# A two-layer network on one core: the order of the second layer's end is rewritten (rows, convolution, pairs, scatters, sums)

## The chip, the core and the metric

The kernel runs on one core of a Trainium2 chip. The metric is the device time of one execution in microseconds (us), shown as the median of several executions. Five engines work in parallel, each through its own queue in order: TensorE (PE; its weight loads are listed as PEld), VectorE (DVE), ScalarE (ACT), GpSimd (POOL) and SyncE (SP), which here only starts transfers. POOL starts the transfers that follow a list of indices. All times inside an execution are counted from the start of the span of the profiled execution.

## What is computed

Four sequences of 1024 tokens with 256 channels in float32 pass through two layers. Layer 0 is causal latent attention with 16 heads and a mixture of 16 experts, two for each token. The change does not touch it. Layer 1, cut to what matters:

```python
# attention: relu, cubed and normalised q and k, kv product, 3-tap convolution over tokens
q = _norm_last(_norm_last(relu(q) + EPS) ** 3)          # the same for k
kv = einsum('bhnd,bhne->bhde', k, v)
z = 1.0 / (einsum('bhnd,bhd->bhn', q, k.sum(axis=2)) + EPS)
out = einsum('bhnd,bhde,bhn->bhne', q, kv, z)
xp = pad(out, ((0, 0), (1, 1), (0, 0)))
out = out + xp[:, 0:N] * w[:, 0] + xp[:, 1:N+1] * w[:, 1] + xp[:, 2:N+2] * w[:, 2] + b_dwc
x = x + ga * (einsum('bnc,oc->bno', out, w_proj) + b_proj)
# experts: one of eight for each token
h = layernorm(x) * (1 + cb) + sb
probs = softmax(h @ router_w + router_b)
x = x + gb * max(probs) * (h @ expert_w[argmax] + expert_b[argmax])
```

## The kernel before

`attention1` goes through five rounds, b = 0 to 4. In a round `front(b)` (layer norm, k and v, the kv products, q) and `back(b - 1)` (the products `ps_o` L1574, their normalisation `on` L1580, transposes `ps_oT` L1589 into `o`, the convolution `y` L1601, the projections `ps_pr` L1609, the sum into x L1614) are advanced in turn. After each turn `k.around.step(pieces, rides)` advances work of the experts that lies beside: *tasks* such as `rows(b)` (statistics of the layer norm, normalised rows `h`, router logits) and `sort(p)`, and *riders* such as `send(p)`. A round's pace says how many sixths of a piece one turn carries: `(6, 8, 6, 6, 12)[b]`, and one ride goes with each step unless another number is given.

The tokens are sorted by expert in three parts: part 0 is the sequences 0 and 1, part 1 is sequence 2 and part 2 sequence 3. `sort(p)` (L882 on) finds each row's place (`index`, L933) and the experts' offsets (`ps_expert` L949). `send(p)` loads rows back from memory (`hs`, L1870) and scatters them 128 at a time into `sorted` (L964), 16 scatters for part 0, 8 for each of the others. The sorted rows are then worked on in 25 pairs of tiles, 11 + 7 + 7. A pair loads `xs` (256 KB, L1008, SP's queue), transposes it (`ps_xT` L1923), copies it out (`xT`, ACT, L1927 for part 0, L1930 with a scale and a shift for the others), multiplies it with its expert's weights (`ps_y` L1938), adds the bias (L1944), for parts 1 and 2 the gate (L1946), and stores `results` (L1947, SP). `combine(p)` gathers the rows back in the order of the tokens (`ys`, L974, POOL, six buffers), scales them (part 0 on ACT, L2002, then gate and sum on DVE, L2007 and L2008; the others in one DVE operation, L1996) and stores `out_dram` (L2010).

The order on each engine comes from the order in which the program gives out instructions and from priorities; `k.pin` fixes an instruction's place among the pinned ones. `k.anchor` names a matmul behind which scatters and gathers are paced. Riders and tasks of parts 0 and 1 run between later pairs, with `k.around.step(2, 2)` after each pair. `count_sums` (L499) checks softmax sums in three passes through `good` tiles, which take buffers with the tag "xs" (six of them, the same as the loads of the pairs); it is given out when part 1's pairs end. `out_of_bounds` (L512) reduces that check with a matmul (`ps_good` L521) when part 2's pairs end.

Of the kernel before, what the change touches and what calls it, by code (L numbers as in the profile page):

```python
# [8 lines left out]
F32 = mybir.dt.float32  # L9
I32 = mybir.dt.int32  # L10
AF = mybir.ActivationFunctionType
ALU = mybir.AluOpType
# [488 lines left out]
def count_sums(k, pool):  # L501

    recs = [k.recs.rearrange("p n i j -> p (n i j)")]
    recs += [k.recs1[:, i].rearrange("p b t h -> p (b t h)") for i in range(2)]
    inverse = 1.0 / SUM_HI, 1.0 / SUM_LO
    for i, (rec, (low, high)) in enumerate(zip(recs, (inverse, (SUM_LO, SUM_HI), inverse))):
        good = pool.tile([P, 8 * B * H], F32, tag="xs", name="good", bufs=6)
        count_within(k, good, rec, low, high, k.good[:, i : i + 1])

# [333 lines left out]
class Sorting:  # L843
# [38 lines left out]
    def sort(self, sel, pool, index, offset):  # L882
# [50 lines left out]
        nc.vector.tensor_scalar(index, rows, 0.0, float(self.most * P - 1), ALU.max, ALU.min)  # L933
        yield 1
# [26 lines left out]
    def scatter(self, rows, buffer, index):  # L961

        tc = self.k.tc
        i = self.k.nc.gpsimd.indirect_dma_start(  # L964
            out=buffer.ap, out_offset=bass.IndirectOffsetOnAxis(ap=index, axis=0),
            in_=rows, in_offset=None, bounds_check=self.most * P - 1, oob_is_err=False,
        ).ins
        for other in buffer.writers:
            tc.declare_no_dep(i, other, reason="their rows are others")
        buffer.writers.append(i)  # L970
        self.paced(i)
# [473 lines left out]
def attention1(ctx, k, a, after_batch=lambda b: None):  # L1445
# [22 lines left out]

    nc.vector.tensor_scalar(dw[:, :, 1], dw[:, :, 1], 1.0, None, ALU.add)
# [86 lines left out]

    def back(b):
        kv, qT = kvs.pop(b), qTs.pop(b)
# [9 lines left out]
        for q in range(2):  # L1568
# [25 lines left out]
            nc.vector.tensor_tensor(xs, xs, bcast(bg, 1, 4), ALU.add)  # L1594
            yield
        for cc in range(CC):
            nc.scalar.activation(
                y[:, cc], o[:, cc, 1 : N + 1], AF.Identity, bias=db[:, cc, :], scale=dw[:, cc, 1:2]
            )
            for j in (0, 2):  # L1600
                nc.vector.scalar_tensor_tensor(  # L1601
                    y[:, cc], o[:, cc, j : N + j], dw[:, cc, j : j + 1], y[:, cc], ALU.mult, ALU.add
                )
            yield
# [12 lines left out]
    k.misc = ps_m  # L1617
    for b in range(B + 1):
        while b == HB and k.awaited in k.around.tasks:
            k.around.step()  # L1620
        todo = ([front(b)] if b < B else []) + ([back(b - 1)] if b else [])
        pace = (6, 8, 6, 6, 12)[b]
        n = 0
        while todo:
            todo = [g for g in todo if next(g, k) is not k]
            n += pace
            k.around.step(n // 6)
            n %= 6
        if b:
            after_batch(b - 1)  # L1630
# [153 lines left out]
class Experts1:  # L1784


    def __init__(self, k, a, out):
# [19 lines left out]
        self.sent = set()  # L1807
# [38 lines left out]
    def sort(self, p):  # L1846
# [12 lines left out]
        yield from sorting.sort(sel, rt, index, offset)  # L1859
        k.around.riders.append(self.send(p, index))  # L1860
        self.state[p] = index, offset, part

    def send(self, p, index):
# [10 lines left out]
        for i in range(len(pairs)):  # L1874
            hs = coming.pop(0)
            if i + 2 < len(pairs):
                coming.append(fetch(*pairs[i + 2]))
            for n in (2 * i, 2 * i + 1):
                self.sortings[p].scatter(hs[:, n % 2], k.sorted1[p], index[:, 0, n : n + 1])
                yield  # L1880
        self.sent.add(p)

    def run(self, early):

        k = self.k
        nc = k.nc
        work = self.back = self.stack.enter_context(
            k.tc.tile_pool(name="f1_work", bufs=2, reuse_waits="tile")
        )
        ps_x = self.stack.enter_context(  # L1890
            k.tc.tile_pool(name="f1_ps_x", bufs=4, space=PSUM, reuse_waits="tile")
        )
        ps_o = self.stack.enter_context(
            k.tc.tile_pool(name="f1_ps_o", bufs=4, space=PSUM, reuse_waits="tile")
        )
        k.misc = ps_x

        pairs = [
            (p, list(range(g, min(g + 2, s.tiles))))
            for p, s in enumerate(self.sortings)  # L1900
            for g in range(0, s.tiles, 2)
        ]
        coming = []

        def fetch(n):

            for p, tiles in pairs[n + len(coming) : n + 5]:
                if p not in self.sent:
                    break
                xs = work.tile([P, 2, C], F32, tag="xs", name="xs", bufs=6)  # L1910
                k.sorted1[p].load(xs[:, : len(tiles)], tiles)
                coming.append(xs)

        def tiles_of(p, tiles, xs):

            n = len(tiles)
            at = self.sortings[p].offsets(
                self.state[p][1], tiles, [mybir.EngineType.PE, mybir.EngineType.DVE]
            )
            ps = ps_x.tile([P, 2, CC, P], F32, tag="m", name="ps_xT")  # L1920
            for j in range(n):
                for cc in range(CC):
                    nc.tensor.transpose(ps[:, j, cc], xs[:, j, cc * P : (cc + 1) * P], k.ident)  # L1923
            xT = work.tile([P, 2, CC, P], F32, tag="xT", name="xT", bufs=3)
            b = PARTS[p][0] if len(PARTS[p]) == 1 else None
            if b is None:
                nc.scalar.copy(xT[:, :n], ps[:, :n])  # L1927
            else:
                for cc in range(CC):
                    nc.scalar.activation(  # L1930
                        xT[:, :n, cc], ps[:, :n, cc], AF.Identity,
                        bias=k.modF[:, cc, b : b + 1], scale=k.modF[:, 2 + cc, b : b + 1],
                    )
            yield
            po = ps_o.tile([P, 2, C], F32, tag="o", name="ps_y")
            for j in range(n):
                for cc in range(CC):
                    k.anchor = nc.tensor.matmul(  # L1938
                        po[:, j], lhsT=xT[:, j, cc], rhs=self.we[:, cc, bass.ds(at[j], C)],
                        start=cc == 0, stop=cc == CC - 1,  # L1940
                    ).ins
            y = work.tile([P, 2, C], F32, tag="y", name="y", bufs=3)
            for j in range(n):
                nc.vector.tensor_tensor(y[:, j], po[:, j], self.be[:, bass.ds(at[j], C)], ALU.add)  # L1944
            if b is not None:
                nc.vector.tensor_tensor(y[:, :n], y[:, :n], bcast(self.gate[:, b], 1, n), ALU.mult)  # L1946
            nc.sync.dma_start(k.results1[p].part(tiles), y[:, :n])  # L1947

        again, before = None, None
        for n, (p, tiles) in enumerate(pairs):  # L1950
            if p not in self.sent and before is not None:
                next(before, None)
                before = None
            while p not in self.sent:
                k.around.step(1, 2)
            fetch(n)
            now = tiles_of(p, tiles, coming.pop(0))
            next(now)
            if before is not None:
                next(before, None)  # L1960
            before = now
            if n + 1 == len(pairs) or pairs[n + 1][0] != p:
                next(before, None)
                before = None
                if early and p + 2 == len(PARTS):
                    count_sums(k, work)
                if early and p + 1 == len(PARTS):
                    again = out_of_bounds(k, work, ps_x)
                k.around.tasks.append(self.combine(p))
            k.around.step(2, 2)  # L1970
        k.around.drain()
        self.stack.close()
        return again

    def combine(self, p):
        k, work = self.k, self.back
        nc = k.nc
        index, _, part = self.state[p]
        most = self.sortings[p].nt

        def fetch(n):
            ys = work.tile([P, C], F32, tag="ys", name="ys", bufs=6)
            self.sortings[p].gather(ys, k.results1[p], index[:, 0, n : n + 1])
            return ys

        coming = []
        for n in range(4):
            coming.append(fetch(n))
            yield 0.5
        for n in range(most):  # L1990
            j = n % 2
            b, t = PARTS[p][n // NT], n % NT
            ys = coming.pop(0)
# [9 lines left out]
            if n + 4 < most:  # L2003
                coming.append(fetch(n + 4))
            if j == 1 and len(PARTS[p]) > 1:
                xs = k.x[b][:, t - 1 : t + 1]
                nc.vector.tensor_tensor(y, y, bcast(self.gate[:, b], 1, 2), ALU.mult)  # L2007
# [10 lines left out]
def two_layers(ctx: ExitStack, tc: tile.TileContext, a: dict, out: bass.AP):  # L2018
# [56 lines left out]
    def stages(first, second, early):  # L2075
# [22 lines left out]
        with ExitStack() as s, tc.using_default_side("right"):  # L2098
# [3 lines left out]
            second(s, k, a, *([after_attention1] if early else []))  # L2102
# [84 lines left out]
```

## Time and profile before

| what | us |
|---|---|
| median of 3 executions | 1086.05 |
| lowest and highest | 1083.16, 1089.41 |
| the profiled execution | 1087.63 |
| its span | 1085.8 |

| moments of the second layer in the profiled execution | us |
|---|---|
| kv products of rounds 1, 2, 3 on DVE (L1548) start | 826.4, 881.6, 934.2 |
| `y` of the convolution of batches 1, 2, 3 ends | 856.4, 906.1, 959.3 |
| `index` of the first sort | 926.2 |
| the 16 scatters of part 0 on POOL | 927.2 to 957.5 |
| first `xs` load issued | 959.1 |
| the last projections | 960.5 to 969.5 |
| scatters of part 2 | 996.4 to 1006.5 |
| gathers of part 0 / part 1 / part 2 | 1010.8 to 1033.0 / 1039.2 to 1050.3 / 1065.1 to 1075.3 |
| last `ps_y` ends | 1059.7 |

The profiled execution lies 1.58 us above the median; 1.83 us of its time lie outside its span. One reads the two tables together: the first says what is to be explained, the second where in the span each step of the end stands. Medians from issue to landing are 4.0 us for `xs`, 3.7 for `ys` and 3.4 for a store to `out_dram`.

### The profile page before, as it was taken

Reading aid. Unit: us, or ns where it says so; the run is one execution under the profiler, and the core shown is the slowest. Engines: PE = TensorE matmul, PEld = TensorE weight load, DVE = VectorE, ACT = ScalarE, POOL = GpSimd, SP = SyncE. Lnnn points to the kernel's source line nnn. Section 1 sums busy time; section 2 is a strip of 40 time slices with the busy share of each in tenths; the row PEclk is TensorE's granted clock in tenths of the full one; section 3 lists DMA queues with packets and bytes.
Section 4 is the critical chain, followed back from the end, with each engine's and each line's share of the span. In section 5 each row is a group of like instructions: output and inputs, shape, how many; then the busy total and the mean of one; then the engine's idle time right before and its main releaser. Section 6 shows DMA issues by size and latency. Waiting matters only on the chain.

```text
span 1085.8 us, 18090 instructions
## 1 busy us (share of the span) xinstructions
PE 945.7 (87%) x6072; PEld 559.8 (52%) x6072; DVE 620.4 (57%) x1987; ACT 602.5 (55%) x959; POOL 336.0 (31%) x528
## 2 busy tenths in 40 slices
PE   4899999999999999889679989986997989858760
PEld 2434434443443434335568878874464656547550
DVE  5822235422465155413676767993899968564572
ACT  0368655765477555775555657766654745523430
POOL 2013211311232234663004615612550100553632
PEclk9999999999999999999899999998999899989875
DMA  6995000100010001552825556624223201458764
GB/s 206 358 346 179 1 1 6 40 1 1 1 64 1 1 30 54 201 215 78 317 88 170 197 177 189 196 75 144 67 65 148 88 2 39 141 170 264 240 205 130
DMA packets 97142, 132.89 MB, mean 122 GB/s; under 512 B 8536, under 2 KB 84216, under 8 KB 96528
## 3 DMA queue, kind: packets, MB, share of 16 engines
q1 hardware_dynamic: 84656, 97.27, 26.9%
q0 software_dynamic: 11776, 33.57, 9.9%
q8 instruction: 52, 0.85, 0.3%
q10 hardware_dynamic: 608, 0.79, 0.3%
q14 instruction: 50, 0.41, 0.1%
HBM read 67.85 MB, written 63.75 MB: 121 GB/s over the span
## 4 chain that ended last, share of the span: by engine, by line
PE 63%; DVE 19%; issue 5%; DMA 5%; ACT 4%; POOL 1%; SPq 1%; DVEq 0%; ACTq 0%; POOLq 0%
PE ps_s L388 13%; PE ps_av L453 12%; PE ps_qk L364 6%; PE ps_y L1312 5%; PE ps_h L1247 4%; PE ps_v L349 3%; PE ps_out L427 3%; PE ps_pr L1609 3%; PE ps_y L1938 3%; PE ps_q L1537 2%; PE ps_k L1511 2%; DVE y L1601 2%; DMA ys<-results,index 2%; PE ps_lnT L1057 1%; DVE st L1258 1%
## 5 line engine op out<-in xcount | busy, mean ns | idle before, releaser
L396 ACT ACTIVATE pT<-ps_s 128x1024 f32<-128x1024 f32 x288 | 279.3, 1022 | 169.7 <-PE ps_s L388 167.2
L399 POOL TENSOR_SCALAR_AFFINE_SELECT pT<-pT 128x256 f32<-128x256 f32 x256 | 104.2, 431 | 328.4 <-ACT pT L396 323.7
L388 PE MATMUL ps_s<-qT,kT 32*128 32x512 f32 (+3 forms) x1536 | 178.8, 523 | 0.1
L453 PE MATMUL ps_av<-pT,v 128*32 128x512 f32 (+3 forms) x1536 | 165.2, 497 | 9.4 <-DVE turned L411 5.6
L964 POOL DMA_INDIRECT sorted<-hs,index x96 | 96.2, 1002 | 144.9 <-PE ps_y L1312 73.0
L974 POOL DMA_INDIRECT ys<-results,index x96 | 102.7, 1070 | 119.0 <-DMA results<-y 43.6
L388 PEld LDWEIGHTS ps_s<-qT,kT 32*128 32x128 f32 x1536 | 74.5, 185 | 95.5 <-issue 72.8
L453 PEld LDWEIGHTS ps_av<-pT,v 128*32 128x32 f32 x1536 | 40.6, 108 | 104.0 <-issue 58.7
L1247 PE MATMUL ps_h<-w,xT 128*128 x352 | 82.1, 386 | 6.5 <-DVE mv L1259 3.8
L1312 PE MATMUL ps_y<-w,act 128*128 x352 | 83.7, 392 | 4.2 <-DVE rs_seed L84 2.8
L411 DVE STREAM_TRANSPOSE turned<-ps_av 128x512 f32<-128x512 f32 x32 | 22.8, 712 | 98.9 <-PE ps_av L453 98.6
L1312 PEld LDWEIGHTS ps_y<-w,act 128*128 128x128 f32 x352 | 67.7, 197 | 14.0 <-ACT act L1295 4.8
L1247 PEld LDWEIGHTS ps_h<-w,xT 128*128 128x128 f32 x352 | 66.2, 193 | 15.9 <-issue 4.2
L1295 ACT ACTIVATE act<-ps_hT,gain 128x128 f32<-128x128 f32 x176 | 63.6, 463 | 16.9 <-PE ps_hT L1286 16.8
L1270 ACT ACTIVATE hid<-hid,nmr,rstd 128x256 f32<-128x256 f32 x88 | 47.5, 603 | 39.4 <-DVE nmr L1263 39.2
L1511 PE MATMUL ps_k<-wqkv,hT 128*128 128x512 f32 x128 | 61.9, 603 | 3.6 <-DMA wqkv<-in_wqkv_dram 2.8
L1938 PE MATMUL ps_y<-we,xT 128*128 x200 | 53.0, 412 | 10.6 <-ACT xT L1930 8.4
L371 DVE COPY qT<-ps_qk 128x512 f32<-128x512 f32 x16 | 11.0, 688 | 81.8 <-PE ps_qk L364 81.8
L103 DVE BATCH_NORM_STATS2 ln_st<-x 128x6 f32<-128x256 f32 x128 | 49.2, 407 | 0.5
L1255 DVE TENSOR_TENSOR hid<-ps_h,b 128x256 f32<-128x256 f32 x88 | 33.9, 415 | 26.6 <-PE ps_h L1247 21.5
L1938 PEld LDWEIGHTS ps_y<-we,xT 128*128 128x128 f32 x200 | 38.2, 204 | 20.1 <-ACT xT L1930 11.6
L374 DVE TENSOR_SCALAR kT<-ps_qk,par 128x512 f32<-128x512 f32 x32 | 22.5, 745 | 37.0 <-PE ps_qk L364 37.0
(223 smaller groups left out, 1499.4 us busy)
## 6 DMA issues: line engine op xcount, KB each, us to landing
xs<-sorted SPq DMA_DIRECT2D x69, 256.0 KB, 3.8
results<-y SPq DMA_DIRECT2D x69, 256.0 KB, 3.0
sorted<-zero SPq DMA_DIRECT2D x2, 6016.0 KB, 20.1
rows_in<-h SPq DMA_DIRECT2D x16, 512.0 KB, 2.9
hs<-rows_in POOLq DMA_DIRECT2D x32, 256.0 KB, 3.5
w<-in_w_dram SPq DMA_DIRECT2D x8, 1024.0 KB, 11.3
x<-in_x_dram SPq DMA_DIRECT2D x4, 1024.0 KB, 6.5
b<-in_b_dram SPq DMA_DIRECT2D x2, 2048.0 KB
```

The costliest lines, as they stand in the source:

```text
L364: nc.tensor.matmul(ps, lhsT=w[:, cc, g * P : (g + 1) * P], rhs=hT[:, cc, hf * 512 : (hf + 1) * 512], start=cc == 0, stop=cc == CC - 1,)
L388: k.anchor = nc.tensor.matmul(pair[hh // 2][:, hh % 2, c0 : c0 + w], lhsT=kTs[o][rows, kb * P : (kb + 1) * P], rhs=qT[rows, q1 - w : q1], ...
L396: nc.scalar.activation(pT, ps, AF.Exp, scale=1.0 / L**0.5)
L399: nc.gpsimd.affine_select(out=pT[:, :, c0 : c0 + P], in_=pT[:, :, c0 : c0 + P], compare_op=ALU.is_ge, fill=0.0, base=0, pattern=[[0, 2], [ ...
L453: nc.tensor.matmul(po[32 * hh : 32 * hh + 32, 512 - w :], lhsT=vs[b % 2][:, kb, 8 * g + 2 * hh + o, :], rhs=exps[b, g, o, u][hh // 2][:, h ...
L964: i = self.k.nc.gpsimd.indirect_dma_start(out=buffer.ap, out_offset=bass.IndirectOffsetOnAxis(ap=index, axis=0), in_=rows, in_offset=None, ...
L974: self.paced(self.k.nc.gpsimd.indirect_dma_start(out=rows, out_offset=None, in_=buffer.ap, in_offset=bass.IndirectOffsetOnAxis(ap=index, a ...
L1247: mm = nc.tensor.matmul(ph[:, j], lhsT=xTs[i // 2][:, j, cc], rhs=w1[:, cc, bass.ds(at[i + j], C)], start=cc == 0, stop=cc == CC - 1,)
L1295: o = nc.scalar.activation(act[:, j, cc], pt[:, j, cc], AF.Gelu, bias=gain[:, 1, cc, t : t + 1], scale=gain[:, 0, cc, t : t + 1],)
L1312: mm = nc.tensor.matmul(po[:, j], lhsT=acts[i // 2][:, j, cc], rhs=w2[:, cc, bass.ds(at[i + j], C)], start=cc == 0, stop=cc == CC - 1,)
L1511: k.anchor = nc.tensor.matmul(ps, lhsT=hT[:, cc, t * P : (t + 1) * P], rhs=wqkv[:, cc, C:], start=cc == 0, stop=cc == CC - 1,).ins
L1938: k.anchor = nc.tensor.matmul(po[:, j], lhsT=xT[:, j, cc], rhs=self.we[:, cc, bass.ds(at[j], C)], start=cc == 0, stop=cc == CC - 1,).ins
```

## The change

1. The addition of one to the middle tap, `dw`, is given out in `back(0)` instead of ahead of the rounds.
2. In the round b = 2 nothing is advanced beside before turn 8, and then at pace 8. In b = 3 the pace is 9. From b = 3 on two riders go with each step.
3. The last batch's convolution is done in halves of 511 and 513 tokens, each inside the loop over halves of the queries, ahead of the next half's products.
4. `beside` is called after each turn of the last round (b = 4). Once part 0 is sent, it loads rows and works on three pairs in turns 8, 9 and 10, in two buffers of the tag "hT" and in the PSUM banks with the tag "p".
5. `sort` calls `ready()` when `index` is written, ahead of the experts' offsets, and this starts `send(p)`. The last part's sender goes ahead of all other riders and isn't paced. `around.step(3.5, 0)` ahead of the pairs and the list `pieces` set how many pieces follow the first pairs.
6. `count_sums` gives out one pass after each of part 0's pairs from the seventh on, and its tiles have the tag "out".
7. The gathers are riders of their own (24 `ys` buffers, three rides after each pair). All combines, all stores to `out_dram` and `out_of_bounds` are given out behind the last pair.

```diff
@@ count_sums
-        good = pool.tile([P, 8 * B * H], F32, tag="xs", name="good", bufs=6)
+        good = pool.tile([P, 8 * B * H], F32, tag="out", name="good")
         count_within(k, good, rec, low, high, k.good[:, i : i + 1])
+        yield
@@ Sorting.sort
         nc.vector.tensor_scalar(index, rows, 0.0, float(self.most * P - 1), ALU.max, ALU.min)
+        ready()
         yield 1
@@ Sorting.scatter
-        self.paced(i)
+        if not at_once:
+            self.paced(i)
@@ attention1
-    nc.vector.tensor_scalar(dw[:, :, 1], dw[:, :, 1], 1.0, None, ALU.add)
...
+    def convolve(o, y, lo, hi):
+        for cc in range(CC):
+            nc.scalar.activation(
+                y[:, cc, lo:hi], o[:, cc, 1 + lo : 1 + hi], AF.Identity,
+                bias=db[:, cc, :], scale=dw[:, cc, 1:2],
+            )
+            for j in (0, 2):
+                nc.vector.scalar_tensor_tensor(
+                    y[:, cc, lo:hi], o[:, cc, j + lo : j + hi], dw[:, cc, j : j + 1], y[:, cc, lo:hi],
+                    ALU.mult, ALU.add,
+                )
+            yield
...
+            if b == B - 1:
+                for _ in convolve(o, y, *((0, N // 2 - 1), (N // 2 - 1, N))[q]):
+                    pass
             yield
...
+        if b < B - 1:
+            yield from convolve(o, y, 0, N)
...
+    k.bank = lambda name: ps_p.tile([P, 2, C], F32, tag="p", name=name)
+    k.spare = lambda: work.tile([P, CC, N], F32, tag="hT", name="spare")
...
-        pace = (6, 8, 6, 6, 12)[b]
+        pace, first = ((6, 0), (8, 0), (8, 7), (9, 0), (12, 0))[b]
         n = 0
+        turn = 0
         while todo:
             todo = [g for g in todo if next(g, k) is not k]
-            n += pace
-            k.around.step(n // 6)
+            turn += 1
+            if turn > first:
+                n += pace
+            k.around.step(n // 6, 1 + b // (B - 1))
             n %= 6
+            if b == B:
+                fill(turn)
@@ the experts of layer 1
-        yield from sorting.sort(sel, rt, index, offset)
-        k.around.riders.append(self.send(p, index))
+        riders = k.around.riders
+        yield from sorting.sort(
+            sel, rt, index, offset,
+            lambda: riders.insert(0 if p + 1 == len(PARTS) else len(riders), self.send(p, index)),
+        )
...
+    def beside(self, turn):
+        if 0 not in self.sent or turn > 10:
+            return
+        if self.space is None:
+            xs, other = (self.k.spare().rearrange("p c (n d) -> p (c n) d", d=2 * C) for _ in range(2))
...
+            self.space, self.most = space, 3
+        self.fetch()
+        if 8 <= turn <= 10:
+            self.pair()
+        if turn == 10:
+            self.products()
...
+        counts = count_sums(k, work) if early else iter(())
+        pieces = [0, 1.5, 3.5, 2.5, 2, 0, 1] if early else []
+        if early:
+            around.step(3.5, 0)
+        while self.done < len(self.pairs):
+            p = self.pairs[self.done][0]
+            if p not in self.sent:
+                self.products()
+            while p not in self.sent:
+                around.step(1, 2)
+            self.pair()
+            if p == 0 and self.done > 6:
+                next(counts, None)
+            if self.done == len(self.pairs) or self.pairs[self.done][0] != p:
+                around.riders.append(self.gathers(p))
+            around.step(pieces.pop(0) if pieces else 2, 3)
+        for _ in counts:
+            pass
+        again = out_of_bounds(k, work, ps_x) if early else None
+        while around.riders:
+            around.step(0)
+        around.tasks += [self.combine(p) for p in range(last + 1)]
+        around.drain()
...
+    def gathers(self, p):
+        index = self.state[p][0]
+        for n in range(self.sortings[p].nt):
+            ys = self.back.tile([P, C], F32, tag="ys", name="ys", bufs=24)
+            self.sortings[p].gather(ys, self.k.results1[p], index[:, 0, n : n + 1])
+            self.got[p].append(ys)
+            yield
```

`pair` fetches up to five pairs ahead, gives out one pair's transposes and copy, and then the products of the pair before it; `products` gives out what is left of that.

## The prediction, made before the changed kernel was run

> **What bounds the kernel now.** I read the page first, then busy time by stretches of the second layer, then what TensorE (PE) waits for there, then PE in order of time near the end, then the chain of waits. Each line quoted is whole.
>
> The page says that PE is busy 87% of the span, and that the last twentieth has no PE at all (the last digits of the row fall to 0).
>
> ```profile
> span 1085.8 us, 18090 instructions
> PE 945.7 (87%) x6072; PEld 559.8 (52%) x6072; DVE 620.4 (57%) x1987; ACT 602.5 (55%) x959; POOL 336.0 (31%) x528
> PE   4899999999999999889679989986997989858760
> ```
>
> Everything before 757 us is the same program, so I cut the rest into stages (busy us of PE, PEld, DVE, ACT, POOL, then granted clock, DMA share, GB/s):
>
> ```profile
> 827.60:866.00 38.40, 28.53 (x164) 20.79 (x163) 37.20 (x120) 24.44 (x46) 3.20 (x8) 0.87 0.44 158
> 936.80:960.40 23.60, 11.03 (x103) 8.68 (x102) 16.15 (x56) 12.69 (x21) 15.38 (x17) 0.86 0.54 173
> 970.00:1000.00 30.00, 24.73 (x159) 18.82 (x158) 14.22 (x68) 12.40 (x23) 11.68 (x14) 1.00 0.74 234
> 1000.00:1043.00 43.00, 33.91 (x159) 27.21 (x157) 27.02 (x55) 18.81 (x40) 25.80 (x25) 0.92 0.76 240
> 1043.00:1062.00 19.00, 10.60 (x38) 8.12 (x38) 13.42 (x32) 3.06 (x6) 5.26 (x6) 0.73 0.65 203
> 1062.00:1086.00 24.00, 0.00 (x0) 0.00 (x0) 3.99 (x10) 0.00 (x0) 8.07 (x8) 0.52 0.39 119
> ```
>
> The reader sees VectorE (DVE) full at 828–866, PE idle half of 937–960, PE with holes from 970 on, and 24 us of gathers and stores at the end. The waits of PE, first 820 to 970, then 970 to 1062:
>
> ```profile
> PE ps_expert L949 <- DVE index L933: 7.7, 1, 7.7
> ```
> ```profile
> PE ps_y L1938 <- ACT xT L1930: 8.4, 4, 3.6
> PE ps_xT L1923 <- DMA xs<-sorted: 6.4, 1, 6.4
> ```
>
> And PE in order of time, with the idle time before each step in brackets:
>
> ```profile
> 1019.01 3.54 PE L1938 MATMUL ps_y<-we,xT 128*128 x8 [3.58 <-ACT xT L1930]
> ...
> 1027.93 2.83 PE L1938 MATMUL ps_y<-we,xT 128*128 x8 [3.22 <-ACT xT L1930]
> ...
> 1048.90 2.30 PE L1923 MATMUL ps_xT<-ident,xs 128*128 128x128 f32 x8 [6.42 <-DMA xs<-sorted]
> 1051.46 3.75 PE L1938 MATMUL ps_y<-we,xT 128*128 x8 [0.26 <-issue]
> ```
>
> Two causes stand behind these holes. ACT's `out` of the combine (L2002) waits for gathered rows and stands ahead of `xT` in ACT's queue. And the xs load was issued only at 1043.34, since the sum check's `good` tiles (L507) use the same buffers: the chain of waits runs through DVE good L495–L498 at 1037–1041 into that load. After the 6.42 us hole the eight matmuls take 3.75 us, not 2.0.
>
> **What the Trainium skill says.** "TensorE: Matmul & The Clock Gate", section "HAM oscillation — how this bites in real kernels", says that an idle gap over about 3.4 us sends the array back to half rate. The trace agrees: 3.75 us after the 6.42 us hole, 3.54 after the 3.58 us one, 1.89 to 2.02 elsewhere. "DMA: Bandwidth & Descriptors", section "Issuing engines are not separate DMA queues", says that transfers issued by sync and gpsimd share the same 16 engines. The trace agrees: at 1002–1008, with pairs and scatters together, the DMA share was 1.02 at 326 GB/s, and xs then landed in 5.0 us (median 1000–1062) against 4.0 over all pairs. "Perfetto Trace Analysis", section "Optimization Strategy", advises interleaving regimes with different limits; the gathers on POOL beside PE's pairs are that, and the trace shows that 24 of 32 were already beside pairs.
>
> **The change part by part.** The sum is against the profiled execution (span 1085.8, time 1087.63, which is 1.58 above the median of 1086.05).
>
> *Rows later in the phase of front(2).* At 826.4–856.4 DVE is busy 29.22 of 30 us, so what is removed before the convolution counts in full. rows(0)'s pieces there (statistics, rsqrt chain, h) are 6.1 us; the work that stays up to the fourth y (L1601, 4 x 1.28) is 22.5 where 28.6 stood. y ends at about 850, not 856.4. But the pieces come back behind it, before or beside the kv products. From y to kv(2) I count 26.4 us of DVE, giving 877–878 against 881.4. Gain 3.5 (2 to 6). front(3) has rows(1) and the whole first sort in it: even, 52 against 52.7. The first sort's `index` comes at about 912.5, 34 us after kv(2), where it came at 926.23.
>
> *Scatters twice as fast, three pairs beside the last projections.* Removed: the 7.7 us wait of ps_expert for index. Added: a wait of PE. PE's queue is in order, and in the new order the first ps_xT of a pair stands behind six of the eight ps_o of the last batch's first half. It waits for all 16 scatters and for the load. POOL issues a scatter each 1.28 us, and a row load (hs) between two of them adds 0.77: 16 x 1.28 + 6 x 0.77 = 25.1; from the last scatter's end to the load's issue 1.5 (957.53 to 959.07), and 4.0 to land: index + 30.6, near 943 (941 to 945; in the kernel before, 36.8). The six ps_o are done at 933. So about 10 us (8 to 12) of new PE wait. Queued behind it are the other ten ps_o, both ps_oT groups, the rows of batch 2 and, through `o`, both halves of the convolution. From 943 on: ps_o, transposes, the half convolution (8 DVE operations, about 0.69 each by the 128x512 row of L1614, 5.5 us in place of 5.1; the extra overhead 0.4 is hidden in the DVE's gaps of this stretch, 16.15 busy of 23.6) take 16 us, projections 8.94, three pairs 3 x 2.17 = 6.5. End near 975, with three pairs done, against 969.5 with none: 5.5 spent, 6.5 earned. Net +1 (loss 2 to gain 4). xs loads for pair 4 stand on SP behind three `results` stores that wait for those pairs, so land at about 980; rows of batch 3 (x at 970.2 before) fill PE meanwhile.
>
> *Last sort closer.* step(3.5,0) ahead of the pairs and the pieces list: its expert product was at 995.9; batch 3's rows start 5 us later, and save about as much by fewer pairs between. I take 996, with 8 pairs done where 7 were. Its eight scatters no longer wait for a matmul, but they were already 1.28 apart (999.09 to 1005.49): worth nothing.
>
> *Sums and combines behind the last pair, good on another tag.* From 996 seventeen pairs remain. At 2.17 us each (seen 996 to 1015) this is 37 us; I put 2.25 for the denser DMA: 38.3, last ps_y at 1035. Before it was 1059.70. Removed are ACT waits 8.4, xs wait 6.4, and the slow matmuls after them (1.5 + 0.9 + 1.7 + 0.5 + 1.9, about 6). The rest is one pair and the shorter early part.
>
> *The tail.* From the last ps_y to the end before: 1059.7 to 1085.8, 26.1 us: results land 4.65, eight gathers at 1.31, landing 3.7, two STT and store 7.9. These eight gathers still wait for the last results. New in the tail: the ACT `out` 16 x 0.5 = 8, DVE 16 x 0.69 = 11 and 16 STT x 0.41, but the last gathered rows only come 15 us after the last pair, so 11 + 3.3 fits into it. Price if that cover goes: up to 8. The stores, 4 MB at 300 GB/s = 14 us, begin 6 us after the last pair and end with the last. I take 27 (26 to 32): span 1062 to 1063.
>
> POOL must have done 24 gathers by 1040: from 1010.8, 24 x 1.31 = 31.4, to 1042. That is a tie, so it costs up to 2. I put the span at 1063, time 1065 for an execution like the profiled one; less 1.58 for the median: 1063.5, and I say **1064**.
>
> Other edits: dw+1 (L1469), for which DVE waits 8.0 us at 757.6 for its load, keeps its slot in DVE's order: nothing, and PE only waits 2.8 us there for wqkv anyway. `ready()` ahead of the offsets lets scatters start some 0.4 us sooner, counted as nothing. Single yields in the count put DVE pieces of about 0.5 us beside pairs, where DVE is busy 27.02 of 43 us, so the rest of it hides them; without that cover three such operations for each of the sums would stand between be-adds, at most 1.7 us a pair while they last.
>
> **Rivals.**
> 1. *The transfers become the bound.* Pairs move 512 KB in 2.17 us = 242 GB/s, gathers 128 KB in 1.31 us = 100; 342 is above the 326 seen at share 1.02. If each pair takes 2.6 us while gathers run, and the tail's stores meet the last gathers: 17 x 0.4 = 6, plus 5: **1075**. For: the share of 1.02. Against: only part of the pairs have gathers beside.
> 2. *The new PE wait is shorter or the pairs fill more.* If scatters end by 938 and the pairs behind them run with PE's holes: **1053**. For: hs loads overlap scatters. Against: POOL's queue is in order.
> 3. *Slower: gathers fall behind the last pair.* Gathers are paced by the last matmul before them and stand on POOL behind the last batch's scatters. If those for part 0 begin only when all pairs are done, 32 x 1.31 = 42 us start at 1041: 1083 + 3.7 + 0.5 + 7.9 = span **1095**. It decides once more than about 25 of the 32 are late. Against: 24 ys buffers and three riders to a pair, and the order of the new program has them among the pairs.
> 4. *The change does little*: the new wait of 10 us at ps_xT grows to over 30, as the scatters share POOL with hs loads that wait for rows_in: **1085**.
>
> **How the numbers follow.** Forecast 1064, own range 1056 to 1072: 0.60. Rival 1: 0.20. Rival 2: 0.07. Rival 3: 0.09. Rival 4: 0.04. The range 1049 to 1078 leaves out rivals 3 and 4 and the edges of the others, where the tail's 5 us and the new wait's 4 us add. 0.5% is 5.4 us, what a measurement of this kernel can tell from no change. Faster are the forecast and rivals 1 and 2, 0.87; rival 4 is the same, 0.04; rival 3 slower, 0.09.
>
> **What would show it.** kv(2) near 878, index(0) near 912; one PE wait at the first ps_xT of 8 to 12 us near 943; projections' end near 975; the last expert product near 996; no wait of ps_y for ACT over 1 us after 1000; the last ps_y near 1036; 26 to 28 us after it. Wrong: a PE wait over 20 us there, pairs of 2.6 us, or the last gathers starting over 10 us after the last results.

## The result, and the profile after

Eight executions of the changed kernel have a median of 1076.74 us (1073.70 to 1079.03), beside 1087.47 for the kernel before on the same chip: a ratio of 0.9903, interval 0.9883 to 0.9924. The forecast was 1064. The change gains 10.7 us, about half of what was forecast. The profiled execution took 1077.86 us, its span is 1076.1. Line numbers below are those of the kernel shown in each fence; for the same operation the changed kernel's are up to 20 higher than before, and some 85 higher in `combine`.

The page of the changed kernel, its span and the row of PE's busy tenths:

```profile
span 1076.1 us, 18091 instructions
PE   4899999999999999899778999987898998786880
```

Each digit is a fortieth of the span: the last one, 27 us, is still without PE. The stages of the changed kernel (length, then busy us of PE, PEld, DVE, ACT, POOL, granted clock, DMA share, GB/s):

```profile
934.00:960.00 26.00, 14.79 (x105) 12.86 (x104) 10.94 (x37) 12.15 (x22) 5.32 (x7) 0.74 0.39 126
972.00:1004.00 32.00, 20.22 (x111) 15.18 (x109) 14.44 (x69) 9.89 (x18) 7.85 (x11) 0.80 0.65 213
1004.00:1044.00 40.00, 39.72 (x215) 34.12 (x214) 26.57 (x59) 15.81 (x31) 27.34 (x28) 0.99 0.84 266
1044.00:1076.00 32.00, 0.31 (x3) 0.09 (x2) 18.71 (x37) 7.15 (x16) 16.24 (x13) 0.58 0.67 214
```

From 1004 to 1044 PE is full: the holes of before are gone, and eighteen pairs run at 2.2 us each. Two stretches are worse than forecast: 972 to 1004, where PE works 20 of 32 us, and the 31.9 us behind the last pair. The waits of PE from 820 on:

```profile
PE ps_xT L1939 <- DMA spare<-sorted: 7.3, 1, 7.3
PE ps_lnT L1060 <- ACT h L1033: 5.2, 1, 5.2
PE ps_rank L896 <- DVE rtotal L819: 5.0, 2, 4.0
...
PE ps_y L1956 <- ACT xT L1948: 0.3, 1, 0.3
```

The wait of ps_y for ACT at parts 1 and 2 went from 8.4 us to 0.3, and the one of 6.4 us for xs is gone. In their place stand the new wait at the first ps_xT, and two waits inside the chain of the last rows. PE in order of time shows where they are:

```profile
941.43 0.87 PE L1939 MATMUL ps_xT<-ident,spare 128*128 128x128 f32 x3 [7.28 <-DMA spare<-sorted]
...
972.34 0.59 PE L1956 MATMUL ps_y<-we,spare 128*128 x2
978.13 0.47 PE L1060 MATMUL ps_lnT<-ident,h 128*128 128x128 f32 x1 [5.20 <-ACT h L1033]
...
982.15 3.01 PE L1956 MATMUL ps_y<-we,xT 128*128 x8 [0.28 <-ACT xT L1945]
985.00 0.60 PE L1060 MATMUL ps_lnT<-ident,h 128*128 128x128 f32 x4
...
998.87 0.66 PE L896 MATMUL ps_rank<-sel,before 128*128 128x64 f32 x2 [3.99 <-DVE rtotal L819]
...
1004.22 0.20 PE L951 MATMUL ps_expert<-past,all 8*1 8x14 f32 x2
...
1040.57 3.62 PE L1956 MATMUL ps_y<-we,xT 128*128 x16
```

The last expert product, the end of the last sort on PE, stands at 1004.22; it was at 995.90. POOL in order of time (last scatters, first gather, and the last eight, which begin at 1051.01):

```profile
1003.78 1.06 POOL L966 DMA_INDIRECT sorted<-hs,index  x1 [10.10 <-DVE mine L949]
...
1013.11 0.97 POOL L966 DMA_INDIRECT sorted<-hs,index  x1 [0.30 <-issue]
1018.81 1.04 POOL L977 DMA_INDIRECT ys<-results,index  x1 [4.73 <-PE ps_xT L1939]
...
1049.52 1.02 POOL L977 DMA_INDIRECT ys<-results,index  x1 [0.30 <-issue]
1051.01 1.47 POOL L977 DMA_INDIRECT ys<-results,index  x1 [0.46 <-ACT out L2087]
...
1061.20 2.86 POOL L977 DMA_INDIRECT ys<-results,index  x1 [0.30 <-issue]
```

From the first gather on POOL has hardly a gap but the 0.3 us between two issues (the longest is 0.46): 45.3 us for 32 gathers. The first gather comes 8.0 us later than before (1018.81 against 1010.81), by about as much as the last sort. The same places in the kernel before, first on PE, then on POOL:

```profile
974.30 0.33 PE L1057 MATMUL ps_lnT<-ident,h 128*128 128x128 f32 x1 [1.72 <-ACT h L1030]
...
995.90 0.19 PE L949 MATMUL ps_expert<-past,all 8*1 8x14 f32 x2 [1.05 <-DVE past L945]
```
```profile
1010.81 1.04 POOL L974 DMA_INDIRECT ys<-results,index  x1 [4.34 <-PE ps_y L1938]
...
1065.12 1.00 POOL L974 DMA_INDIRECT ys<-results,index  x1 [14.78 <-DMA results<-y]
...
1074.33 1.00 POOL L974 DMA_INDIRECT ys<-results,index  x1 [0.31 <-DVE x L1996]
```

### The profile page after: what moved, and what is told of

Read it like the earlier page. It is cut to its first block, busy times and chain, and to the rows that moved or that the text cites. A ratio compares the mean times of both kernels' runs of the same rounds, so it can differ in the third digit from the quotient of the medians.

```text
span 1076.1 us, 18091 instructions
## 1 busy us (share of the span) xinstructions
PE 947.2 (88%) x6072; PEld 563.0 (52%) x6072; DVE 618.1 (57%) x1991; ACT 603.6 (56%) x961; POOL 336.6 (31%) x528
## 5 line engine op out<-in xcount | busy, mean ns | idle before, releaser
L1512 PE MATMUL ps_k<-wqkv,hT 128*128 128x512 f32 x128 | 65.3, 628 | 3.3 <-DMA wqkv<-in_wqkv_dram 2.8
L1956 PE MATMUL ps_y<-we,xT 128*128 x176 | 44.6, 401 | 0.6 <-ACT xT L1948 0.3
L1324 DVE TENSOR_TENSOR y<-ps_y,b 128x256 f32<-128x256 f32 x88 | 35.2, 418 | 15.0 <-PE ps_y L1315 14.8
```

Source lines behind the costliest of these rows:

```text
L1512: k.anchor = nc.tensor.matmul(ps, lhsT=hT[:, cc, t * P : (t + 1) * P], rhs=wqkv[:, cc, C:], start=cc == 0, stop=cc == CC - 1,).ins
```

## The experiments

The theory after the first profile was that, with all sums behind the last pair, the end is set by POOL. POOL needs 32 gathers (42 us at 1.31) from the moment when part 0's eleven pairs are done, or 40 issues (52 us) from the last index, whichever is later, and then some 12 us to land, add and store. What makes either moment late was to be found: the wait at the first ps_xT, the order of pairs and rows, the pass of the sum check in the last sort. The rival was that the tail is long because stores and gathers collide behind the last pair. A second rival was not stated: that the end still follows PE, since the last eight gathers need the results of the last pair. The traces of the same runs decide between it and POOL, below.

Times are compared as ratios to the kernel before on the same chip. The changed kernel, measured a second time, is the measure:

> The changed kernel itself, as the measure for the others of this call. On an undisturbed chip 0.990 of the kernel before, last index near 1003 and first gather near 1019 in the profile; if the kernel before takes about 1097 us again, the ratio tells what such a chip makes of the change.

It gave 0.9902 (0.9881 to 0.9923): the same.

**Pairs held back.** The order on PE has the first pair's transposes ahead of ten of the sixteen `ps_o`. `k.pin` ties an instruction to the one given out just before it on its engine. Here, as I read the code, that is the pair's own load of its offsets, so it holds nothing back. This kernel ties the transposes to the last `ps_oT` (order of issue only):

```diff
-                    nc.tensor.transpose(
+                    k.hold = nc.tensor.transpose(
                         pt[:, i * P : (i + 1) * P], on[:, i, cc * P : (cc + 1) * P], k.ident
-                    )
+                    ).ins
...
+                if self.most < len(self.pairs):
+                    k.tc.add_manual_dep(
+                        tr.ins, k.hold.name,
+                        mybir.DependencyInfo(mybir.DependencyClass.NoSync, mybir.DependencyReason.DATA),
+                        reason="behind the last transposes",
+                    )
```

> The changed kernel, with the transposes of the three pairs beside the projections kept behind the last batch's last ps_oT (order of issue only). Theory: the end hangs on the time at which part 0's eleven pairs are done, since 32 gathers then run on POOL without a gap; what moves that moves the end one to one. Then the wait of 7.3 us at the first ps_xT goes, the projections end near 966 instead of 972.8, the first gather starts near 1012 instead of 1018.8, and the kernel takes 6 to 7 us less than the changed one (about 1070 where that took 1076.7). Rival: DVE fills this stage, the wait comes back as a wait for the convolution, and at most 2 us are gained.

Measured 1070.24 us, ratio 0.9822 (0.9791 to 0.9853): below the changed kernel's interval, the fastest of all. PE in order of time in this kernel:

```profile
951.96 1.04 PE L1607 MATMUL ps_oT<-ident,on 128*128 128x128 f32 x8
952.83 0.93 PE L1939 MATMUL ps_xT<-ident,spare 128*128 128x128 f32 x7
```

The bracket with the wait is gone, and the projections end at 968.0, 4.5 us sooner, though the first sort's scatters started 3.4 us later in this execution. The time fell by the ratio's 0.8%, 8.7 us, about the whole wait. Three of the kernels below hold the pairs back and change one thing more. Each has a partner measured beside it that has that other thing alone, and takes less than its partner by 7.1 us (one piece behind each pair), 6.9 us (late passes) and 5.7 us (late passes again, among the runs set apart below); in none of these couples do the intervals overlap. So the hold is worth 6 to 9 us, and the rival's limit of 2 us is passed each time.

**No pairs beside the projections.** The call of `beside` is left out, so that all 25 pairs come behind:

```diff
-            second(s, k, a, *([after_attention1, experts1.beside] if early else []))
+            second(s, k, a, *([after_attention1] if early else []))
```

> The changed kernel without the three pairs beside the projections (no call of beside; all 25 pairs behind). Theory (the wait at ps_xT costs more than the three pairs bring): projections end near 960, the last expert product near 992, the eleventh pair ends 3 to 8 us sooner, the first gather starts at 1011 to 1016, and the kernel takes 3 to 8 us less than the changed one. Rival (the pairs are worth their 6.5 us of PE): the eleventh pair is as late or later, and the time is 0 to 4 us more than the changed one.

Measured 0.9901 (0.9863 to 0.9938): no difference. The time is the rival's, the first gather (1015.6) the theory's. The three pairs, as the change places them, bring about what their wait costs. POOL in this kernel:

```profile
1002.88 0.97 POOL L966 DMA_INDIRECT sorted<-hs,index  x1 [0.30 <-issue]
1015.61 1.42 POOL L977 DMA_INDIRECT ys<-results,index  x1 [11.75 <-DMA xs<-sorted]
```

The last sort is done 10.6 us sooner than in the changed kernel (expert product at 993.59), and POOL then stands 11.75 us, since the eleventh pair isn't done. So a closer last sort alone doesn't move the end, nor does a first gather that comes 3 us sooner.

**Pairs sooner, sort later.** The opposite: one piece behind each pair, with and without the pairs held back.

```diff
-        pieces = [0, 1.5, 3.5, 2.5, 2, 0, 1] if early else []
+        pieces = [1] * 12 if early else []
```

> The changed kernel with one piece of the last rows and the last sort behind each pair (a list of twelve ones in place of [0, 1.5, 3.5, 2.5, 2, 0, 1]), so that the pairs of part 0 come sooner and the last sort later. Theory (the end hangs on part 0's eleventh pair, not on the last sort): the first gather starts at 1008 to 1012 instead of 1018.8, although the last expert product comes later than 1004; since eight scatters now fall among the gathers (8 x 1.28), only part of it is kept, and the kernel takes 1 to 4 us less than the changed one. Rival (the last sort decides): the last expert product is 2 to 5 us later, and so is the end.

> Both: the pairs beside the projections behind the last ps_oT, and one piece behind each pair. Theory: the gains add, the first gather starts at 1002 to 1006, and the kernel takes 8 to 11 us less than the changed one (1066 to 1069). Rival (the last sort decides): it takes as long as the kernel with the transposes held back alone, or longer.

Measured 0.9927 (0.9903 to 0.9952) and 0.9862 (0.9837 to 0.9887): the first gains nothing, and the second takes no less than with the pairs held back alone, as its rival said. POOL in the first, then PE:

```profile
1006.07 1.05 POOL L966 DMA_INDIRECT sorted<-hs,index  x1 [19.90 <-DVE index L934]
1007.42 1.06 POOL L977 DMA_INDIRECT ys<-results,index  x1 [0.30 <-issue]
...
1019.15 0.98 POOL L966 DMA_INDIRECT sorted<-hs,index  x1 [0.30 <-issue]
1020.43 1.05 POOL L977 DMA_INDIRECT ys<-results,index  x1 [0.30 <-DMA sorted<-hs,index]
...
1051.85 1.50 POOL L977 DMA_INDIRECT ys<-results,index  x1 [2.49 <-ACT out L2087]
```
```profile
1024.81 0.63 PE L1939 MATMUL ps_xT<-ident,xs 128*128 128x128 f32 x4 [3.21 <-DMA xs<-sorted]
...
1028.45 1.08 PE L1939 MATMUL ps_xT<-ident,xs 128*128 128x128 f32 x4 [3.02 <-DMA xs<-sorted]
```

The eleventh pair is early enough that gathers stand among the scatters without a gap, but a scatter is the first of the 40 and waits 19.90 us for the last index. The first gather comes 11 us sooner than in the changed kernel, and the end does not move. Two lines show why. The late scatters make later pairs wait for their rows, 3.2 and 3.0 us on PE, so the last pair ends at 1045.2 and not sooner than in the changed kernel (1044.2). And POOL, which is ahead now, stands 2.49 us before the 25th gather, the first that needs the last pair: the trace has the last results landing at 1050.86, 1.0 us before it, and the `out` named in the bracket is also given out behind the last pair. Here PE's last pair sets the end, not POOL. With the pairs held back as well POOL stands there for 2.39 us.

**Rows of the last batch ahead of the pairs**, so that both lnT groups stand before pairs 4 and 5:

```diff
-            around.step(3.5, 0)
+            around.step(4.5, 0)
```

> The changed kernel, with 4.5 instead of 3.5 pieces given out ahead of the pairs behind the projections, so that both lnT groups of the last rows stand ahead of the transposes and products of pairs 4 and 5. Theory: pairs woven into the chain of the last rows and the last sort make that sort late; the last expert product then comes near 1000.5 instead of 1004.2, the first gather 3 us sooner, the end 3 us sooner (1073 to 1074). Rival: the pairs are put off by as much, the eleventh pair ends where it did, and the time is that of the changed kernel within 1 us.

Measured 0.9916 (0.9889 to 0.9942), the rival's case. From the last rows' statistics (L1026 on DVE) to the last index it takes 24.3 us, in the changed kernel 26.1, before 22.0; the first gather still comes at 1019.25. The two ends of this chain on DVE, before and in the changed kernel:

```profile
973.45 0.17 DVE L1023 SCALAR_TENSOR_TENSOR ln_mv<-ln_mv,ln_rstd 128x8 f32<-128x8 f32 x1
...
995.47 0.15 DVE L933 TENSOR_SCALAR index<-rows 128x8 int32<-128x8 f32 x1
```
```profile
977.28 0.17 DVE L1026 SCALAR_TENSOR_TENSOR ln_mv<-ln_mv,ln_rstd 128x8 f32<-128x8 f32 x1
...
1003.33 0.15 DVE L934 TENSOR_SCALAR index<-rows 128x8 int32<-128x8 f32 x1
```

**The pass of the sum check.** The first pass (L495 to L498, 2.2 us on DVE) falls between the last rows' logits and the last sort. Here the passes stand behind pairs 14 to 16:

```diff
-            if p == 0 and self.done > 6:
+            if p == 1 and self.done > 13:
                 next(counts, None)
```

> The changed kernel with the three passes of the sum check behind pairs 14 to 16 instead of pairs 7 to 9, beside the changed kernel itself. Theory (the pass of 2.2 us on DVE inside the chain of the last sort is a cause of its lateness, and POOL's work from the last index on sets the end): last index 2 us sooner counted from the end of the projections, time 1 to 3 us less than the changed kernel. Rival: 0 within 1 us, since the index comes sooner but the eleventh pair doesn't.

> The pairs beside the projections held behind the last ps_oT and the passes of the sum check behind pairs 14 to 16. Theory: 7 to 10 us less than the changed kernel beside it. Rival: the wait comes back elsewhere, under 4 us less.

Measured 0.9928 (0.9905 to 0.9951) alone, which is the rival's case in that nothing is gained, and 0.9865 (0.9840 to 0.9891) with the pairs held back, 4.0 us less than the changed kernel and short of the theory's 7. The longest wait of PE for the last sort's first product is 2.5 us instead of 4.0, in this line of the first kernel's waits:

```profile
PE ps_rank L896 <- DVE part L1886: 2.5, 1, 2.5
```

From the statistics to the last index it takes 25.5 us, 1.4 less than in the changed kernel measured beside it (26.9), and the time doesn't fall: the first gather comes 5.8 us after the last scatter's end instead of 4.9, and POOL then stands 2.38 us before the 25th gather. Where POOL would have gained, first the eleventh pair and then the last one hold it.

**Sums given out as before.** Each combine behind its part's last pair:

```diff
                 around.riders.append(self.gathers(p))
+                around.tasks.append(self.combine(p))
...
-        around.tasks += [self.combine(p) for p in range(last + 1)]
```

> The changed kernel with each part's combine given out behind that part's last pair, as in the kernel before, not all behind the last pair. Theory of the prediction: ACT's out stands ahead of xT again, and PE waits for xT some 8 us in all, so that the last ps_y comes 6 to 8 us later; since the gathers on POOL run beside it, the end moves 0 to 4 us. Rival: with 24 ys buffers the gathers are ahead, out no longer waits, PE waits for xT under 2 us, and the stores come off the end: 2 to 5 us less.

Measured 1.0069 (1.0043 to 1.0094), 18 us more than the changed kernel and worse than either side expected. The waits of PE from 1000 to 1060, then of ACT from 1000 on:

```profile
PE ps_y L1956 <- ACT xT L1948: 13.2, 4, 8.8
```
```profile
ACT out L2087 <- DMA ys<-results,index: 20.6, 10, 12.5
```

`out` waits for the gathers ahead of `xT`, PE waits for `xT`, and the last eight gathers wait for the last pair (last ps_y at 1058.9). The 24 `ys` buffers don't prevent it. So this part of the change, too, is worth more than the whole gain once the others are in place: the parts' worths can't be added up.

**Rows not held back.**

```diff
-        pace, first = ((6, 0), (8, 0), (8, 7), (9, 0), (12, 0))[b]
+        pace, first = ((6, 0), (8, 0), (6, 0), (6, 0), (12, 0))[b]
```

> The changed kernel with the old paces 6 and 6 in rounds 2 and 3 and no rows held back in round 2. By the prediction's sum: the convolution of batch 1 ends 5 us later again, the kv products of round 2 come 2 to 4 us later, the first sort's index about 10 us later, the wait at the first ps_xT grows by as much, and the kernel takes 5 to 10 us more than the changed one. Rival: the pieces held back come in the next round and cost there what they saved: within 2 us of the changed one.

Measured 1.0002 (0.9991 to 1.0014): without this part (the delay in round 2 and the paces of rounds 2 and 3) the whole gain is gone, 10.9 us. The first ps_xT in this kernel:

```profile
953.51 0.69 PE L1939 MATMUL ps_xT<-ident,spare 128*128 128x128 f32 x2 [12.96 <-DMA spare<-sorted]
```

The index of the first sort comes 12.4 us later (924.39 against 911.97), and everything behind it follows: first ps_xT 12.1 later, last expert product 8.2, first gather 8.2.

**The convolution in one piece.**

```diff
-            if b == B - 1:
-                for _ in convolve(o, y, *((0, N // 2 - 1), (N // 2 - 1, N))[q]):
-                    pass
             yield
-        if b < B - 1:
-            yield from convolve(o, y, 0, N)
+        yield from convolve(o, y, 0, N)
```

> The changed kernel with the last batch's convolution in one piece. By the prediction's sum the halves bring 2 to 3 us here, since the whole convolution would stand behind the second half's transposes. Rival: within 1 us of the changed kernel beside it, as DVE waits in this stage anyway.

Measured 0.9910 (0.9889 to 0.9931), the rival: the halves bring nothing that can be told.

**Half of the stores left out.** The four stores of part 0 to `out_dram` are dropped, so this kernel writes half of the output:

```diff
-            if t % 4 == 3:
+            if t % 4 == 3 and len(PARTS[p]) == 1:
```

> The changed kernel, without the four stores of part 0's rows to out_dram (half of the output is not written). Theory of the end alone (eleventh pair, then 32 gathers at 1.31): nothing changes but the last microsecond, 0 to 1 us less. Rival: the stores that the change puts behind the last pair slow the last eight gathers and their landing; then these start 1.3 us apart instead of 1.6 and land in 2.5 us instead of 3.4, and the kernel takes 4 to 5 us less (1072).

Measured 0.9884 (0.9858 to 0.9909), 2 us less with overlapping intervals, between the two expectations. The last eight gathers take 12.4 us from the first's start to the last's end, against 13.1 in the changed kernel and 10.2 before. So these stores are not the main cause of the slower gathers. From the last gather's end to the end of the span it takes 9.2 us, against 11.1 to 12.8 in the eleven other profiles of these groups whose sums stand behind the last pair, and 10.5 before: there, in this one profile, the stores do seem to count.

**Runs with other waits.** Two further groups of runs fell where the kernel before took 1097 us, and where PE, ACT and DVE of these kernels stood for 4 to 11 us at a time between 1010 and 1055, most often released by nothing that this core's trace shows. ACT in the second run of the pairs held back (the bracket has the idle time ahead):

```profile
1026.74 1.02 ACT L1954 ACTIVATE xT<-ps_xT,modF 128x256 f32<-128x256 f32 x2 [5.44 <-remote]
1036.85 1.93 ACT L1954 ACTIVATE xT<-ps_xT,modF 128x256 f32<-128x256 f32 x4 [9.09 <-remote]
```

> The pairs beside the projections held behind the last ps_oT, once more. If the whole wait of 7.3 us reaches the end, 0.983 to 0.985 of the kernel before; if half of it, 0.987.

> The same with four pairs beside the projections instead of three. Theory: the eleventh pair comes sooner, POOL's gap between the last scatter and the first gather shrinks from 5 to about 3 us, and 0 to 2 us are gained over three pairs. Rival: the fourth pair's 2.2 us on PE delay the last rows and the last sort by as much, and 0 to 2 us are lost.

They measured 0.9976 (0.9946 to 1.0006) and 0.9982 (0.9955 to 1.0010). In the other group the check's late passes gave 1.0036, the one-piece convolution 1.0033, and the pairs held back with late passes 0.9984 with three and 1.0014 with four pairs. The changed kernel itself was in neither group. Two kernels that differ from it little, with late passes and with the one-piece convolution, were 0.3% slower than the kernel before there, with intervals above 1, so it is likely that the change's gain is lost in such runs. What held the engines and what a fourth pair brings are open.

## Why the prediction was wrong

Each step against the profiled execution of the changed kernel:

| step | forecast | measured |
|---|---|---|
| kv products of round 2 | 877 to 878 | 875.4 |
| first index | 912.5 | 912.0 |
| new wait at the first ps_xT | 8 to 12, near 943 | 7.3, to 941.4 |
| projections' end | 975 | 972.5 |
| last expert product | 996 | 1004.2 |
| last ps_y | 1035 | 1044.2 |
| from there to the end | 27 | 31.9 |

The first four steps hold within 3 us (the new wait is just under its range), and so do the removed waits: ps_y for ACT 0.3 us instead of 8.4, xs none, no slow matmuls behind them. The pairs run at 2.2 us with the gathers beside them, so the first half of rival 1, pairs of 2.6 us, fell; its second half, 5 us more at the tail, is what came, though the cause it gave, the stores, is shown only in part. Rival 2's first half came true as well (the last of the 16 scatters ended at 937.0), its time did not. "Net +1 (loss 2 to gain 4)" for the pairs beside the projections held: leaving them out changed nothing. Rival 3 fell: the gathers began 25 us before the last pair ended. The direction was right and the gain was put at twice its size. Two terms of the sum carry the miss: 9.2 us in the last pair, 4.9 in the tail, 14 in all against the bare sum of 1062.

**The step that failed first** is "batch 3's rows start 5 us later, and save about as much by fewer pairs between. I take 996, with 8 pairs done where 7 were." They saved nothing. The last sum into x came 3.0 us later (972.56 against 969.51), the statistics took 0.8 longer with the third pair's bias sums among them, and the chain from there to the last index took 26.1 us instead of 22.0. Nor did the "rows of batch 3" fill PE while pair 4 was loading: PE stood 5.20 us ahead of their first transpose, 1.72 before. Of the 4 us in the chain, two causes show in single profiles: the products of a pair between the two lnT groups (24.3 us without) and the pass of the sum check (25.5 without, against 26.9). The same kernel gave 26.1 and 26.9 in its two profiles, so these sizes are rough, and neither edit brought the end forward. The rest is argued only. Seven pairs were done by then, not eight. This term is 8.2 us, and the pairs behind it 1.0.

**The second** is the tail, "I take 27 (26 to 32)": it was 31.9. The sum took the tail from the last ps_y as before, and put the sums and stores behind the last pair at nothing, since all of it "fits into it". Is the end then set by POOL? The profiled executions answer:

| kernel | first gather | wait before the 25th | first gather to the end | last ps_y to the end |
|---|---|---|---|---|
| before | 1010.8 | 14.8 | 75.0 | 26.1 |
| changed | 1018.8 | 0.5 | 57.3 | 31.9 |
| pairs held back | 1015.5 | 0.3 | 57.0 | 31.9 |
| one piece behind each pair | 1007.4 | 2.5 | 69.3 | 31.5 |
| both of these | 1002.9 | 2.4 | 69.0 | 31.3 |
| sums as before | 1015.3 | 11.8 | 77.1 | 33.5 |
| held back, other waits | 1013.7 | 13.4 | 76.3 | 32.8 |

"First gather plus 57" fits only where the gathers begin behind the last scatter and nothing else holds the pairs (56.0 to 59.3 in ten profiles). "Last pair plus 32" fits every profile with the sums behind the last pair: 30.8 to 33.0 in twelve, 31.0 to 33.7 in the six with other waits. POOL and PE come to the last eight gathers almost together: in eight of the twelve the 25th gather starts 1.0 us after the last results landed (in the changed kernel at 1051.01, after 1050.02), and in the other four POOL is late by 0.2 to 2.6 us. So the prediction's "tie" was read rightly: PE's last pair still sets the end, but for these 2.6 us at most.

What made the tail 5.8 us longer than before can be read in three pieces. From the last ps_y to the 25th gather it is 6.8 us instead of 5.4, since the last results landed later. The eight gathers took 13.1 instead of 10.2. From there to the end it is 12.0 instead of 10.5. In the second piece one gather stands out, 2.86 us instead of 1.0 (at 1061.20). DVE at that time:

```profile
1057.56 5.62 DVE L2081 SCALAR_TENSOR_TENSOR x<-ys,part,x 128x256 f32<-128x256 f32 x14
```

These are the sums of part 2 and part 1 into x. As they all stand behind the last pair, fourteen find their rows ready and run without a gap, to 1063.2. All eighteen profiles with the sums behind the last pair have such a run of 12 to 14, and in each one gather, one of the last three, begins within the run, takes 2.5 to 3.7 us, and ends 0.2 to 0.9 us after the run does (0.9 in twelve of them). Gathers begun earlier in the run take 1.2 to 1.3 us. The kernel before and the one with the sums given out as before have no such run, since each sum there waits for its gather; their last eight gathers take 1.0 to 1.1 us each. The reading of the check's flag by POOL falls among the last eight gathers in those two kernels too (at 1070.6 and 1075.7), so it alone isn't the cause. That the run of sums holds the gather up is what the times point to; it is not shown, since no experiment changed the run alone. What else lengthens the third piece, beyond the stores, is open.

The size of single parts was also misjudged. "Gain 3.5" for the held rows was about right for the kv products (round 2's come 50.9 us after round 1's instead of 55.2), but the part's worth is in the first index, 12 us sooner: with the pairs and scatters of the changed kernel behind it, the whole gain hangs on it. One reading was too short as well: the prediction gave slow matmuls after holes of 6.42 and 3.58 us and "1.89 to 2.02 elsewhere", but its own line at 1027.93 has 2.83 us after a hole of 3.22.

## What to carry to other kernels

When work is moved off one queue's path, follow every queue behind it to the end of the kernel: here each wait that was to go did go, but PE stood in the chain of the last rows instead, and the work put behind the last pair lengthened the tail. Shortening the last sort or bringing part 0's pairs sooner, one without the other, gained nothing in four experiments; taking the wait at the first transpose out of PE's queue gained 6 to 9 us. When two rules fit most runs ("first gather plus 57", "last pair plus 32"), look for the runs where they differ: here the kernels whose gathers came early decided. A tie for order has to name the instruction that matters: look at the order that results, and ask what stands behind an instruction that waits.

## What the runs showed of the hardware

Pairs and gathers together moved 266 GB/s at a DMA share of 0.84 without slowing PE: xs landed in 4.9 us (median 970 to 1062) and the loads were far enough ahead. The forecast put 2.25 us to a pair for it; 2.17 to 2.2 was seen.

Indirect transfers of 128 rows that POOL issues one behind another start 1.28 us (scatters) to 1.31 us (gathers) apart. In all eighteen profiles in which DVE makes 12 to 14 `scalar_tensor_tensor` sums without a gap, one gather begun beside them took 2.5 to 3.7 us. In the two that have no such run, the last eight took 1.0 to 1.1 us each.

The clock behaved as the prediction quoted it from the Trainium skill ("TensorE: Matmul & The Clock Gate", section "HAM oscillation — how this bites in real kernels"). After the 5.20 us hole at 978 the eight ps_y at 982 took 3.01 us instead of 1.89, after the 3.99 us hole at 999 those at 1000.67 took 3.62, and the granted clock was 0.80 in that stage. The kernel before shows 2.83 us after 3.22 us without work, so in this case a hole slightly under the page's 3.4 us cost something too. A wait in the chain of the last rows so costs PE twice.
